# Rotary tables of units 2 to 7: by way of memory, two units at a time, or by spreading products on TensorE

## The chip, the cores and the metric

The kernel runs on one core of a Trainium2 chip. The core has five engines with instruction streams of their own: TensorE (PE; its weight loads are listed apart as PEld), VectorE (DVE), ScalarE (ACT), GpSimd (POOL) and SyncE (SP), which in this kernel issues every DMA. They share an on-chip memory of 128 partitions (SBUF) and a small accumulator memory for TensorE's results (PSUM, used here in banks of 512 numbers per partition). A DMA moves data between SBUF and the chip's memory, which the code calls DRAM; the core has 16 DMA engines. The metric is the device time of one execution in microseconds (us), the median of several runs; lower is better. All arithmetic is in 32-bit floats.

## The reference

The input x is 32 sequences of 64 tokens with 512 features. It passes two blocks. Block 0 is a rotary attention with 8 query heads of 64 features and one key and value head, followed by an MLP with a SiLU gate and 2048 inner features. Block 1 is a latent attention with 16 heads of 32 features. Both normalise their input and scale it by a product of the condition `cond_2048`. Cut to what matters for the change:

```python
def apply_rope(x, pos_ids):                       # block 0, HD = 64
    half = HD // 2
    inv_freq = 1.0 / ROPE_BASE ** (jnp.arange(0, HD, 2) / HD)      # 32 frequencies
    ang = pos_ids.astype(jnp.float32)[:, :, None] * inv_freq
    cos = jnp.concatenate([jnp.cos(ang), jnp.cos(ang)], axis=-1)[:, None]
    sin = jnp.concatenate([jnp.sin(ang), jnp.sin(ang)], axis=-1)[:, None]
    x1, x2 = (x[..., :half], x[..., half:])
    return x * cos + jnp.concatenate([-x2, x1], axis=-1) * sin

# block 0
h = ada_rms(x, time_emb, ln1_w, ln1_tw)
q, k = apply_rope(heads(h @ Wq.T), pos_ids), apply_rope(heads(h @ Wk.T), pos_ids)
x = x + softmax(q k^T / 8) v @ Wo.T
h = ada_rms(x, time_emb, ln2_w, ln2_tw)
x = x + (silu(h @ Wg.T) * (h @ Wu.T)) @ Wd.T
# block 1
x = x + latent_attention(layernorm(x) * (1 + scale) + shift) @ Wo.T
```

The positions are an input, so the cosines and sines have to be computed from them in the kernel: for each sequence, token and frequency one cosine and one sine.

## The kernel before, in words

**Units.** The 2048 tokens are worked on in 8 units of 256 tokens, four sequences each (`US` is 4, `S` is 64, `UT` is 256). A unit passes `attention0` (block 0's attention), `mlp` and `second`, which runs `attention1` (block 1). Features lie on the partitions and tokens along the free axis, so that a projection is a row of TensorE products with the weights as the stationary side.

**The MLP.** The inner features are worked on in 8 columns per unit, 64 columns q in all. For each there are three weight sets: m = 0 for the gate, m = 1 for up, m = 2 for down. Each product of a set is done by a scheme that needs seven block products in place of eight and some sums of blocks. `first_products` and `last_products` issue the products of gate and up (`product`, L937) and the sums of their results on DVE and ACT; `gated` makes the gated activations on DVE and POOL; `down` issues the products of the down set (L996). A set is a tile of [128, 7, 256] numbers in one of five buffers (`mw`). In unit 0 three of its seven blocks are loaded with one DMA (L251), one more with another (L254), the other four are summed from these on DVE and POOL (`combine`, L264 to L267) and written to memory (L272). From unit 1 on a set takes two loads, L251 (384 KB) and L256 (512 KB), which fetches those four blocks. The next set is asked for in `done_with`, when the last product of an older one has been issued, so its load waits on SP until that buffer is free.

**The rotary tables.** `angles(u0)` computes cosines and sines for two units at once from the positions: some two dozen DVE operations, two Sin activations on ACT and a last DVE product with a sign (L370). Its result, `angle` [128, 2, 512], stands by frequency and sequence: partition b·32 + f holds frequency f of sequence b of every unit, which leaves 64 tokens per unit along the free axis. The rotation needs something else: all 256 tokens of the unit along the free axis, and on every partition the frequency that belongs to its feature. `spread_out` makes this with four TensorE products with matrices of zeros and ones (L409), one for each sequence, which write a bank of PSUM. `tables(u, r)` calls it for units 2 to 7 and has DVE multiply the cosines (L418) and the sines with their sign (L419) with the normalisation `r` into a tile `cs`; these two operations read PSUM. Then `rotate` uses `cs` on the query and `attention0` on the keys. Units 0 and 1 have their own way (`first_angles`, `tables_by_quarters`), which stays as it is.

**When this happens.** The angles of units 2 and 3 are computed at the end of `attention0` of unit 1, those of 4 and 5 at the end of that of unit 3, those of 6 and 7 at the end of that of unit 5: they are passed as `late`, which `attention0` calls behind its last step. In the profiled execution the last operation of the angles ran at 85.4, 400.4 and 635.0 us, and the products of unit 2's tables began at 165.5 us, those of unit 7's at 771.8 us.

**The order.** Each job (the MLP of unit u, `attention0` of unit u + 1, the chain of `second`) is a generator that yields pairs of cost and latency. `Order.run` always takes the ready job that has done the smallest part of its total, so the costs in the yields decide how the steps of the jobs are interleaved. The order in which operations are issued is handed to the Tile framework, which orders each engine's stream by it and by its own priorities, and places tiles in SBUF, where tiles of different names can share memory at different times. An engine runs its stream in order. All DMAs stand in SP's one stream: weight sets, x, the sums of unit 0's sets, positions and results. A transfer that has to wait holds up those behind it.

Of the kernel before, what the change touches and what calls it, by code (L numbers as in the profile page):

```python
# [10 lines left out]
F32 = mybir.dt.float32  # L11
I32 = mybir.dt.int32
AF = mybir.ActivationFunctionType
ALU = mybir.AluOpType
# [3 lines left out]
P = 128  # L18
B, S, D = 32, 64, 512
# [3 lines left out]
US = UT // S  # L23
# [4 lines left out]
HD0, HALF0 = 64, 32  # L28
HD1, HALF1 = 32, 16
# [82 lines left out]
def two_blocks(ctx: ExitStack, tc: tile.TileContext, a: dict, out: bass.AP):  # L112
    nc = tc.nc
# [3 lines left out]
    dram = ctx.enter_context(tc.tile_pool(name="dram", bufs=1, space=bass.MemoryType.DRAM))  # L117
# [4 lines left out]
    def bank(tag, name):  # L122
        return psum.tile([P, 512], F32, tag=tag, name=name, bufs=BANKS[tag])
# [4 lines left out]
    def abank(name):  # L128
        tags = homes["now"]
        homes["n"] += 1  # L130
        return bank(tags[homes["n"] % len(tags)], name)
# [4 lines left out]
    def fixed(shape):  # L136
        n, i = int(np.prod(shape[1:])), stays["at"]
        stays["at"] += n
        assert stays["at"] <= STAY
        t = stays["all"][:, i : i + n]  # L140
        if len(shape) == 2:
            return t
        names = "abc"[: len(shape) - 1]
        return t.rearrange(f"p ({' '.join(names)}) -> p {' '.join(names)}", **dict(zip(names, shape[1:])))

    def work(tag, shape, name, bufs=2):
        return wk.tile(shape, F32, tag=tag, name=name, bufs=bufs)
# [19 lines left out]
    for q in range(US):  # L167
        rows = slice(q * HALF0, (q + 1) * HALF0)
        for i in range(2):
            block = ident[rows, rows][:, i * HALF1 : (i + 1) * HALF1].unsqueeze(1).unsqueeze(1)  # L170
            to = spread[rows, q].rearrange("p (r a h f) -> p r a h f", r=2, a=2, h=2)[:, :, i]
# [10 lines left out]
    def load_positions(u0):  # L182
        t = work("pos", [P, 2 * S], f"pos_{u0}", 1).bitcast(I32)
        nc.sync.dma_start(t, a["pos"][:, u0 * S : (u0 + 2) * S])
        positions.append(t)
# [9 lines left out]
    sign_of = small[:, C_SIGN:C_ALL]  # L195
# [12 lines left out]
    angle = fixed([P, 2, NU * S])  # L208
# [120 lines left out]
    def angles(u0):  # L329

        cols = slice(u0 * S, (u0 + 2) * S)

        def some(tag, name, cols=512, bufs=2):
            return work(tag, [P, cols], f"{name}_{u0}", bufs)[:, : 2 * S]

        posi = positions.pop()
        posf, sign = some("u", "posf"), some("v", "sign")
        ang, lo, hi = (some(f"ang{i}", f"ang{i}", 2 * S, 1) for i in range(3))
        prod = some("r0", "prod", UT, 1)
        acc, rnd = angle[:, 0, cols], angle[:, 1, cols]  # L340
        nc.vector.tensor_copy(posf, posi)
        nc.vector.tensor_scalar(sign, posf, 0.0, None, ALU.is_ge)
        nc.vector.tensor_scalar(sign, sign, 2.0, -1.0, ALU.mult, ALU.add)
        nc.vector.tensor_tensor(posf, posf, sign, ALU.mult)
        nc.vector.tensor_scalar(ang, posf, freq, None, ALU.mult)
        nc.vector.scalar_tensor_tensor(lo, ang, 4097.0, ang, ALU.mult, ALU.subtract)
        nc.vector.scalar_tensor_tensor(hi, ang, 4097.0, lo, ALU.mult, ALU.subtract)
        nc.vector.tensor_tensor(lo, ang, hi, ALU.subtract)

        def fraction(dst, src):  # L350
            nc.vector.tensor_scalar(rnd, src, ROUND, ROUND, ALU.add, ALU.subtract)
            nc.vector.tensor_tensor(dst, src, rnd, ALU.subtract)

        first = True
        for piece, turn in ((hi, 0), (hi, 1), (lo, 0), (hi, 2), (lo, 1)):
            nc.vector.tensor_scalar(prod, piece, TURN[turn], None, ALU.mult)
            if first:
                fraction(acc, prod)
                first = False
            else:  # L360
                fraction(prod, prod)
                nc.vector.tensor_tensor(acc, acc, prod, ALU.add)
        nc.vector.scalar_tensor_tensor(acc, lo, TURN[2], acc, ALU.mult, ALU.add)
        nc.vector.scalar_tensor_tensor(acc, ang, TURN[3], acc, ALU.mult, ALU.add)
        fraction(prod, acc)
        nc.vector.tensor_scalar(lo, prod, 0.25, None, ALU.add)
        fraction(hi, lo)
        nc.scalar.activation(acc, hi, AF.Sin, scale=TWO_PI)
        nc.scalar.activation(rnd, prod, AF.Sin, scale=TWO_PI)
        nc.vector.tensor_tensor(rnd, rnd, sign, ALU.mult)  # L370
        if u0 + 2 < NU:
            load_positions(u0 + 2)

# [32 lines left out]
    def spread_out(ps, of):  # L406

        for b in range(US):
            nc.tensor.matmul(ps[..., b, :], spread[:, b], of, start=True, stop=True)  # L409

    def tables(u, r):

        ps = abank(f"tab_{u}").rearrange("p (i b s) -> p i b s", i=2, s=S)
        spread_out(ps, angle[:, :, u * S : (u + 1) * S])
        cs = work("cs", [P, 2, UT], f"cs_{u}", 1)
        cos, sin = cs[:, 0], cs[:, 1]
        ps = ps.rearrange("p i b s -> p i (b s)")
        nc.vector.tensor_tensor(cos, ps[:, 0], r, ALU.mult)  # L418
        nc.vector.scalar_tensor_tensor(sin, ps[:, 1], sign_of, r, ALU.mult, ALU.mult)  # L419
        return cos, sin  # L420

    def tables_by_quarters(u, few, room):

        r = few[:, 0]
        nc.vector.tensor_tensor(
            few[:, 1:3], angle[:, :, u * S : (u + 1) * S], r.unsqueeze(1).to_broadcast([P, 2, S]), ALU.mult
        )
        ps = abank(f"tab_{u}").rearrange("p (i b s) -> p i b s", i=2, s=S)
        spread_out(ps, few[:, 1:3])
        pr = abank(f"row_{u}")[:, :UT]  # L430
        spread_out(pr.rearrange("p (b s) -> p b s", s=S), r)
        cs = work("cs", [P, 2, UT], f"cs_{u}", 1)
        ps = ps.rearrange("p i b s -> p i (b s)")
        nc.scalar.copy(cs[:, 0], ps[:, 0])
        nc.scalar.mul(cs[:, 1], ps[:, 1], sign_of)
        row = space(room, "r", UT, f"r_a{u}")
        nc.scalar.copy(row[HD0:], pr[HD0:])
        return cs[:, 0], cs[:, 1], row
# [14 lines left out]
    def space(room, tag, columns, name):  # L453

        if tag in room:
            return room[tag].pop(0)[:, :columns]
        if tag == "few":
            return work({"0": "tot0", "1": "kr1"}[room["ring"]], [P, columns], name, 1)
        return work(tag + room["ring"], [P, columns], f"{name}", RING.get(tag, RING.get(tag + room["ring"], 1)))
# [45 lines left out]
    def rms(u, s, h, room, name):  # L505

        x = x_units[u]
        lean = "lean" in room
        sq = tile4(room, "h", f"sq_{name}") if lean else work("sq", [P, KC, UT], f"sq_{name}", 1)
        nc.scalar.activation(sq, x, AF.Square)  # L510
        if lean:
            parts = [sq[:, k] for k in range(KC)]
            c = KC // 2
            for e, part in ((nc.vector, slice(0, c)), (nc.gpsimd, slice(c, KC))):
                to = h[:, part].rearrange("p c (b s) -> p c b s", s=S)
                of = x[:, part].rearrange("p c (b s) -> p c b s", s=S)
                by = s[:, part, US * u : US * (u + 1)].unsqueeze(3).to_broadcast([P, c, US, S])
                e.tensor_tensor(to, of, by, ALU.mult)
            yield 0.0, 1.5
        else:  # L520
            parts = [total_of(room, sq, name)]
            nc.gpsimd.tensor_tensor(by_seq(h), by_seq(x), per_seq(s, u), ALU.mult)
            yield 0.0, 6.0
        if lean:
            return parts
        r = space(room, "r", UT, f"r_{name}")
        inverse_root(mean_of(parts, f"ms_{name}"), eps0, r)
        return r
# [67 lines left out]
    def attention0(u, room, early=None, late=None):  # L596
        kb, vb = kblk0[u % 2], vblk0[u % 2]
        lean = "lean" in room
# [24 lines left out]
        r = yield from norm  # L623
# [9 lines left out]
        if lean:  # L633
            cos, sin, r = tables_by_quarters(u, few, room)
        else:
            cos, sin = tables(u, r)
        yield 1.0, 0.0

        qT = tile4(room, "qT", f"qT0_{u}")
        turn = turn or query(0)  # L640
# [34 lines left out]
        if lean:  # L675
            ps = [space(room, "p", 512, f"p0_{u}_{t}") for t in range(2)]
        else:
            both = space(room, "p", 1024, f"p0_{u}")
            ps = [both[:, t * 512 : (t + 1) * 512] for t in range(2)]

        for ts in ((0,), (1,)) if lean else ((0, 1),):
            banks = [abank(f"sc0_{u}_{ts[0]}_{r}")[:, : 256 * len(ts)] for r in range(2)]
            for n in range(KC * len(ts)):
                t, c = ts[n // KC], n % KC
                for b in range(2):
                    cols = slice((2 * t + b) * S, (2 * t + b + 1) * S)
                    for r, sc in enumerate(banks):
                        of = slice(r * HD0, (r + 1) * HD0)
# [7 lines left out]
            p = ps[ts[0]] if lean else both  # L696
# [39 lines left out]
        r = yield from rms(u, s0b, h, room, f"b{u}")  # L736
        if lean:
# [3 lines left out]
            r = abank(f"row_b{u}")[:, :UT]  # L741
# [512 lines left out]
```

## Time and profile before

Three runs took 1048.55, 1048.79 and 1049.76 us; the median is 1048.79. The profiled execution took 1047.82 us; its span, from the first to the last instruction, is 1046.0 us, at a mean granted TensorE clock of 0.992.

| engine | busy us | share of the span | instructions |
|---|---|---|---|
| PE | 1007.5 | 96% | 8578 |
| PEld | 936.4 | 90% | 8578 |
| DVE | 548.7 | 52% | 1379 |
| ACT | 334.1 | 32% | 683 |
| POOL | 436.4 | 42% | 521 |

| DMA | KB each | count | median us from issue to landing |
|---|---|---|---|
| set from `in_wmlp` | 384 | 192 | 4.7 |
| set from `sums` | 512 | 168 | 5.7 |
| sums from set | 512 | 24 | 4.8 |
| a from `in_wmlp` | 128 | 24 | 3.1 |

The DMA queue of SP carried 197.17 MB in 68752 packets, 54.5% of the time of the 16 DMA engines. A row of the groups gives the source line, the engine, the operation, the tile written and the tiles read, the shapes and the count, then the busy time and the mean duration in ns, then the idle time of the engine just before and what ended it. A matmul of 32-bit floats shows as two records.

### The profile page before, as it was taken

Reading aid. Unit: us, or ns where it says so; the run is one execution under the profiler, and the core shown is the slowest. Engines: PE = TensorE matmul, PEld = TensorE weight load, DVE = VectorE, ACT = ScalarE, POOL = GpSimd, SP = SyncE. Lnnn points to the kernel's source line nnn. Section 1 sums busy time; section 2 is a strip of 40 time slices with the busy share of each in tenths; the row PEclk is TensorE's granted clock in tenths of the full one; section 3 lists DMA queues with packets and bytes.
Section 4 is the critical chain, followed back from the end, with each engine's and each line's share of the span. In section 5 each row is a group of like instructions: output and inputs, shape, how many; then the busy total and the mean of one; then the engine's idle time right before and its main releaser. Section 6 shows DMA issues by size and latency. Waiting matters only on the chain.

```text
span 1046.0 us, 21558 instructions
## 1 busy us (share of the span) xinstructions
PE 1007.5 (96%) x8578; PEld 936.4 (90%) x8578; DVE 548.7 (52%) x1379; ACT 334.1 (32%) x683; POOL 436.4 (42%) x521
## 2 busy tenths in 40 slices
PE   7899999999999998999999999999999999999987
PEld 6679989998999998999999989899999899999875
DVE  4966656454355376444664366652465425543372
ACT  5333112244123242143340342242323512333141
POOL 3424545544244532445342354324553334642351
PEclk8989999999999999999999999999999999999999
DMA  8816886553655563673646646446745547565201
GB/s 279 314 60 202 275 299 244 195 175 144 230 198 185 171 213 125 233 247 104 229 163 231 233 141 212 160 155 219 259 165 193 180 167 250 185 235 202 79 1 40
DMA packets 68850, 198.53 MB, mean 190 GB/s; under 512 B 7312, under 2 KB 16272, under 8 KB 68368
## 3 DMA queue, kind: packets, MB, share of 16 engines
q1 hardware_dynamic: 68752, 197.17, 54.5%
q8 instruction: 68, 1.11, 0.4%
q14 instruction: 30, 0.25, 0.1%
HBM read 180.37 MB, written 16.78 MB: 188 GB/s over the span
## 4 chain that ended last, share of the span: by engine, by line
PE 81%; DVE 8%; POOL 4%; DMA 4%; issue 2%; ACT 1%; SPq 0%; ACTq 0%; DVEq 0%; POOLq 0%
PE gu L937 33%; PE down L996 16%; PE q L535 10%; PE po L535 10%; DMA set<-in_wmlp 3%; PE sc L875 2%; PE pp L570 1%; PE cx L902 1%; PE lat L535 1%; PE sc L689 1%; PE kv L535 1%; PE cx L710 1%; DVE set L264 1%; DVE sm L563 1%; DMA x<-in_x 1%
## 5 line engine op out<-in xcount | busy, mean ns | idle before, releaser
L937 PE MATMUL gu<-h,set 128*128 128x128 f32 x2048 | 288.6, 277 | 6.8 <-DVE c L956 6.3
L937 PEld LDWEIGHTS gu<-h,set 128*128 128x128 f32 x2048 | 259.4, 193 | 16.2 <-issue 11.3
L937 PE MATMUL gu<-hc,set 128*128 128x128 f32 x1536 | 215.7, 276 | 0.0
L937 PEld LDWEIGHTS gu<-hc,set 128*128 128x128 f32 x1536 | 193.9, 193 | 1.0 <-issue 0.6
L975 POOL TENSOR_TENSOR act<-c,c 128x384 f32<-128x384 f32 x64 | 66.4, 1037 | 212.1 <-DVE c L963 138.2
L996 PE MATMUL down<-td,set 128*128 128x128 f32 x1024 | 137.7, 276 | 3.7 <-POOL td L978 2.5
L996 PEld LDWEIGHTS down<-td,set 128*128 128x128 f32 x1024 | 125.5, 192 | 5.7 <-POOL td L978 3.5
L949 ACT COPY e<-gu 128x128 f32<-128x128 f32 x128 | 33.7, 264 | 260.9 <-PE gu L937 244.9
L535 PE MATMUL po<-cT,stays 128*128 128x256 f32 x480 | 109.4, 382 | 3.4 <-DVE x L583 1.8
L535 PE MATMUL q<-h,stays 128*128 128x256 f32 x480 | 109.4, 381 | 0.0
L996 PE MATMUL down<-act,set 128*128 128x128 f32 x768 | 109.4, 278 | 0.0
L963 DVE TENSOR_TENSOR c<-gu,u 128x256 f32<-128x256 f32 x128 | 53.4, 419 | 106.5 <-PE gu L937 106.2
L951 DVE TENSOR_TENSOR u<-e,gu 128x128 f32<-128x128 f32 x128 | 36.1, 282 | 129.7 <-ACT e L949 129.1
L535 PEld LDWEIGHTS po<-cT,stays 128*128 128x128 f32 x480 | 89.7, 192 | 15.9 <-DVE x L583 2.6
L996 PEld LDWEIGHTS down<-act,set 128*128 128x128 f32 x768 | 97.7, 192 | 5.3 <-issue 3.2
L535 PEld LDWEIGHTS q<-h,stays 128*128 128x128 f32 x480 | 90.1, 191 | 12.3 <-issue 0.4
L565 POOL TENSOR_TENSOR p<-p,sm 128x512 f32<-128x512 f32 x40 | 41.6, 1058 | 121.5 <-DVE sm L564 115.6
L546 POOL TENSOR_TENSOR qT<-u_q,v_q 128x512 f32<-128x512 f32 x30 | 38.1, 1270 | 89.0 <-DVE v_q L545 88.9
L1032 ACT ACT_TABLE_LOAD x35 | 44.9, 1283 | 55.6 <-DVE c L963 55.1
L589 DVE TENSOR_TENSOR x<-x,po 128x512 f32<-128x512 f32 x28 | 19.2, 687 | 72.9 <-PE po L535 72.9
L977 POOL TENSOR_TENSOR td<-act 128x256 f32<-128x256 f32 x64 | 46.7, 730 | 5.6 <-DVE act L974 0.9
L1032 ACT ACTIVATE c<-gu 128x128 f32<-128x128 f32 x64 | 17.7, 277 | 85.6 <-DVE c L963 77.7
(264 smaller groups left out, 1336.6 us busy)
## 6 DMA issues: line engine op xcount, KB each, us to landing
set<-sums SPq DMA_DIRECT2D x168, 512.0 KB, 5.7
set<-in_wmlp SPq DMA_DIRECT2D x192, 384.0 KB, 4.7
sums<-set SPq DMA_DIRECT2D x24, 512.0 KB, 4.8
x<-in_x SPq DMA_DIRECT2D x8, 512.0 KB, 5.6
mod<-in_mod SPq DMA_DIRECT2D x7, 512.0 KB, 5.4
a<-in_wmlp SPq DMA_DIRECT2D x24, 128.0 KB, 3.1
out_x<-x SPq DMA_DIRECT2D x12, 256.0 KB, 2.6
stays<-in_wo SPq DMA_DIRECT2D x2, 1024.0 KB, 8.0
```

Of the source, the lines that this page charges most:

```text
L535: nc.tensor.matmul(ps, w[:, k, cols], h[:, k, :], start=(k == 0), stop=(k == KC - 1))
L546: nc.gpsimd.tensor_tensor(dst, u, v, ALU.add)
L565: nc.gpsimd.tensor_tensor(p8, p8, sm.unsqueeze(2).to_broadcast(wide), ALU.mult)
L875: nc.tensor.matmul(sc[b * S : (b + 1) * S, j * P : (j + 1) * P], qT[of, j, cols], kb[of, 2 * t + b].rearrange("p g k -> p (g k)"), start=True,
L937: nc.tensor.matmul(ps, w[:, slot, k * P : (k + 1) * P], b[of][:, k], start=start and k == 0, stop=k == 1, skip_group_check=True)
L949: nc.scalar.copy(e, ps[:, 0])
L951: nc.vector.tensor_tensor(u2, e, ps[:, 1], ALU.add)
L963: nc.vector.tensor_tensor(c.rearrange("p (a b) t -> p a b t", b=2)[:, :, 1], ps[:, 2:4], u2.unsqueeze(1).to_broadcast([P, 2, HT]), ALU.add,)
L975: nc.gpsimd.tensor_tensor(act[:, 1:4], gate[:, 1:4], c[:, 1:4], ALU.mult)
L977: nc.gpsimd.tensor_tensor(td[:, 0:2], act[:, 1:3], act[:, 0:2], ALU.subtract)
L996: nc.tensor.matmul(sums_of[u][p][:, c], w[:, slot, c * P : (c + 1) * P], b[of], start=q % NP == 0 and i % 2 == 0 and c == 0, stop=q % NP = ...
L1032: nc.scalar.activation(gate[2][:, 0], gate[0][:, 0], AF.Silu)
```

## The change

`angles(u0)` now ends with a call of a new function, `spread_table(u0)`. It makes a tile in DRAM, `rows` [32, 2, 4, 128], with the frequency in front, and fills it with four DMAs, one for each sequence b, from the partitions b·32 to b·32 + 31 of `angle` (32 KB each). Then it reads the tile back with four DMAs of 128 KB into a work tile `table` [128, 2, 4, 128] in SBUF. Each of them fills 32 partitions: it takes 16 frequencies, and a leading dimension of step 0 repeats them for two copies. The reads follow the writes in memory, so the first of them has to wait until all four writes have landed. The table holds two units, 128 tokens for each of the four sequences.

`tables(u, r)` takes its half of this tile in place of the PSUM bank and no longer calls `spread_out`; the two DVE operations read SBUF, and their operands are rearranged to [128, 4, 64]. The step of `attention0` that follows has the planner's cost 0.0 in place of 1.0, except in the units 0 and 1. All new DMAs are issued by SP: 8 for two units, 24 in all.

```diff
@@ angles(u0)
         nc.scalar.activation(rnd, prod, AF.Sin, scale=TWO_PI)
         nc.vector.tensor_tensor(rnd, rnd, sign, ALU.mult)
+        spread_table(u0)
         if u0 + 2 < NU:
             load_positions(u0 + 2)
@@
+    spread_tables = {}
+
+    def spread_table(u0):
+
+        rows = dram.tile([HALF0, 2, US, 2 * S], F32, tag=f"table{u0}", name=f"table{u0}")
+        for b in range(US):
+            nc.sync.dma_start(rows[:, :, b], angle[b * HALF0 : (b + 1) * HALF0, :, u0 * S : (u0 + 2) * S])
+        t = work("table", [P, 2, US, 2 * S], f"table_{u0}", 1)
+        for i in range(4):
+            of = rows[i % 2 * HALF1 : (i % 2 + 1) * HALF1].rearrange("f i b s -> f (i b s)")
+            to = t[i * HALF0 : (i + 1) * HALF0].rearrange("p i b s -> p (i b s)")
+            nc.sync.dma_start(to, of.unsqueeze(0).to_broadcast([2, HALF1, 8 * 2 * S]))
+        for u in range(2):
+            spread_tables[u0 + u] = t[..., u * S : (u + 1) * S]
+
     def tables(u, r):
 
-        ps = abank(f"tab_{u}").rearrange("p (i b s) -> p i b s", i=2, s=S)
-        spread_out(ps, angle[:, :, u * S : (u + 1) * S])
+        ps = spread_tables.pop(u)
         cs = work("cs", [P, 2, UT], f"cs_{u}", 1)
         cos, sin = cs[:, 0], cs[:, 1]
-        ps = ps.rearrange("p i b s -> p i (b s)")
-        nc.vector.tensor_tensor(cos, ps[:, 0], r, ALU.mult)
-        nc.vector.scalar_tensor_tensor(sin, ps[:, 1], sign_of, r, ALU.mult, ALU.mult)
+        r, to = r.rearrange("p (b s) -> p b s", s=S), cs.rearrange("p i (b s) -> p i b s", s=S)
+        nc.vector.tensor_tensor(to[:, 0], ps[:, 0], r, ALU.mult)
+        nc.vector.scalar_tensor_tensor(to[:, 1], ps[:, 1], sign_of, r, ALU.mult, ALU.mult)
         return cos, sin
@@ attention0
-        yield 1.0, 0.0
+        yield 1.0 if lean else 0.0, 0.0
```

## The prediction

> **What bounds the kernel now.** I read the chain of waits first, then the groups of instructions, then the table by stage, and last the single DMAs and instructions around the three places where the change puts transfers. The first answer is the page of the kernel before, its engine totals and its chain:
>
> ```profile
> PE 1007.5 (96%) x8578; PEld 936.4 (90%) x8578; DVE 548.7 (52%) x1379; ACT 334.1 (32%) x683; POOL 436.4 (42%) x521
> PE 81%; DVE 8%; POOL 4%; DMA 4%; issue 2%; ACT 1%; SPq 0%; ACTq 0%; DVEq 0%; POOLq 0%
> ```
>
> TensorE is busy for 96% of the span and carries 81% of the chain, so an instruction taken from it inside the steady part should come off the end. The groups, with shapes kept apart, price what is removed and what reads it (total us, mean ns, idle before it):
>
> ```profile
> L409 PE MATMUL tab<-stays 128*128 128x128 f32 x48 | 6.3, 273 | 0.0
> L418 DVE TENSOR_TENSOR cs<-tab,r_a 128x256 f32<-128x256 f32 x6 | 2.5, 417 | 0.2
> L265 DVE TENSOR_TENSOR set<-set 128x256 f32<-128x256 f32 x22 | 10.5, 476 | 0.0
> ```
>
> 48 records in six units are eight records per unit, back to back with no idle before them: 6.3 us of pure TensorE time, 1.05 us a unit. The table by stage (window, its length, busy us and count of PE, PEld, DVE, ACT, POOL, granted clock, DMA share, GB/s) shows where a late weight load can hurt:
>
> ```profile
> 50.00:100.00 50.00, 47.31 (x428) 42.06 (x431) 33.10 (x94) 17.35 (x35) 17.13 (x19) 0.90 0.37 127
> 100.00:165.00 65.00, 61.96 (x566) 60.69 (x567) 37.96 (x112) 9.71 (x30) 29.80 (x41) 1.00 0.87 294
> 530.00:660.00 130.00, 127.65 (x1035) 119.66 (x1034) 73.75 (x185) 40.59 (x80) 55.96 (x65) 1.00 0.57 193
> ```
>
> PE loses 3.0 us between 100 and 165, where the DMA engines are 87% busy; later they have room. From 165 to 980 us PE idles 9.3 us in all (815 less the busy times of the windows). SP, which issues every DMA in order, stands nearly always for a weight buffer, as its waits say (us in total, times, longest):
>
> ```profile
> SPq L251 <- PE gu L937: 518.7, 117, 30.4
> SPq L251 <- PE down L996: 100.6, 59, 11.3
> ```
>
> So each set is asked for when its buffer falls free. How late that is: the down set of gate column 39 is issued at 640.39 us, lands at 645.10 and is first used by PE at 646.45; the timeline shows the issue and the use:
>
> ```profile
> 640.39 0.33 SPq L251 DMA_DIRECT2D set<-in_wmlp  x1
> ```
>
> ```profile
> 646.45 0.61 PE L996 MATMUL down<-act,set 128*128 128x128 f32 x4
> ```
>
> Its slack is 1.35 us. I took the slack of the other sets in the same way: the down sets of unit 0 have 3.18 us (issued 91.82, landed 94.85, used 98.03), then 1.91, 1.0, 1.3, 0.33, 0.2 and 1.61; the one issued at 416.46 has 3.45; gate and up sets 5 to 19.
>
> **What the Trainium skill says.** "DMA: Bandwidth & Descriptors", section "Why a DMA increments its semaphore by 16 and not by 1": a DMA runs on k engines, the largest k up to 16 that divides the slowest dimension of both access patterns, and on the lowest-numbered ones. Its section "Rules for kernel authors" draws the case at hand: a leading zero-stride broadcast of c copies "confines the whole DMA to at most c engines". The new read has a source of [2 copies, 16 frequencies, 1024 values], so k would be 2. No run here shows it: every load of before has 128 partitions outermost. Section "Queues, rings and completion order": each engine takes descriptors in ring order, so what SP issues later queues behind on those two engines; the trace of before shows no such case either. Section "Anatomy of one DMA — SWDGE (gpsimd) path" puts most of about 2 us fixed time into the write's receipt; the nearest row agrees, 128 KB of the a tile land 3.1 us after issue at the median.
>
> **The change, part by part.** Removed: four spreading products per unit in units 2 to 7, 6.3 us of PE; nothing of the kind replaces them on PE. Where PE is not waiting this is all gain: −6.3.
>
> The two DVE products that make cos and sin stay, and read SBUF in place of PSUM: 417 ns to at most the 476 ns of the SBUF-only row, +0.06 us times 12. DVE is half idle: 0, and 0.7 us if that cover is gone.
>
> Added per pair of units: four writes of 32 KB and four reads of 128 KB, 24 DMAs in all, all on SP. An issue costs SP about 0.33 us (the timeline row above): 2.6 us a pair, beside waits of hundreds. The first read must wait until all four writes have landed, and holds up whatever SP has behind it. Size: 0.64 MB a pair, 1.9 MB beside 197 MB. Spread over 16 engines a read is 8 KB per engine; on two it is 64 KB each, sixteen packets of 4,096 bytes, which last 159 ns each in the trace at the median: 2.54 us a read, 10.2 us for four, on the same two engines, and every later set load ends behind them. I take two engines (chance 0.65), and keep sixteen as the other end.
>
> First pair (units 2 and 3, angles done at 85.7 us). In the compiled order the four writes stand among the combines of the first weight sets, then read 0, then the down set with 3.18 us of slack, two more loads, then read 1; reads 2 and 3 come at about 155 us, behind the load of the set with 1.61. Read 0 can go at about 92.1 us, so that set is issued 0.7 late and lands 2 to 3 us late, beyond its slack only just; read 1 adds 2.54 us for the set with 1.91. Together I take 1.5 us of PE stall, between 0.5 and 3. For reads 2 and 3, the next sets have 5.0 to 7.0 us: 0.3, between 0 and 1.
>
> Second pair (units 4 and 5, angles done at 400.7). The table's memory is shared with small MLP tiles, free at about 403.5; reads follow at about 404 and end, with about 2 us of receipt, near 416.2 on two engines. The cos product ran at 413.50, so DVE stands up to 2.8 us with products of the MLP queued behind it. PE reaches the data of that column only at about 420: 0.8 us, between 0 and 2.
>
> Third pair (units 6 and 7, angles done at 635.3). The writes land at about 639.3; three reads go then, ahead of the down set above. Two engines take 7.6 us for them, to about 647.5, then the set's own share (eight packets of 3,072 bytes at 121 ns and eight of 4,096, 2.2 us) and the receipt: it lands near 650 instead of 645.1. Less its slack of 1.35, PE stalls 3.5 us, between 1.5 and 5.5.
>
> The planner gets 0.0 in place of 1.0 as the cost of that step, so in units 1 to 6 attention pieces stand at other places between MLP products (the order of unit 0's products up to its last columns and of the tail is unchanged), and an added Sin table load of 1.28 us falls on ACT, which is 32% busy. Bound: reordering can recover at most the 9.3 us that PE idles there; a loss is of the size of the largest such wait, 6.3 us for DVE's c products in the whole run. I take 0, and 2.5 either way.
>
> Sum: −6.3 + 1.5 + 0.3 + 0.8 + 3.5 = −0.2. On the profiled execution of 1047.82 us (span 1046.0) that is 1047.6; the median of runs lies 0.97 above that execution, so 1048.6.
>
> **Rivals.** Hidden transfers: the reads run on all engines, or the two engines drain sooner. Then read and set share the bandwidth, only SP's later issue at the third pair stays (0.8 us against the slack of 1.35): −6.3 + 0.8 = −5.5, 1043.3. For it: DMA share 0.57 in the third place. Against: the divisor rule.
>
> Slower, by backlog in unit 0: between 92 and 165 us the two engines have 13% of 65 us, 8.5 us, to spare, and the next down sets have 0.2 to 1.9 us. If the 5.1 us of reads 0 and 1 are never drained before the tightest set, PE pays 4.9 instead of 1.5: +3.2, 1052.0. It decides once this stretch costs over 3.8 us (with the other 4.6 that is the gain plus 2.1). For it: share 0.87 and slack 0.2; against: half of the engines' time is free just before 100.
>
> That the products removed were not on the path, so that nothing is gained and little lost, is hardly possible with 0.0 idle before them; it would also end near 1048.
>
> **How the numbers follow.** A change under 0.2%, 2.1 us, can't be told from none here. Balanced: 0.42, of that faster 0.13, same 0.18, slower 0.11 (reordering of 2.5 and stall bounds). Hidden: 0.36, of that faster 0.32, same 0.04. Backlog: 0.20, all slower. Not on the path: 0.02, same. Faster 0.45, same 0.24, slower 0.31. The range takes in the hidden case with half a us below it and the backlog with 2 us above for the third pair's upper bound: 1042.5 to 1054; the balanced case alone is 1045 to 1051.5.
>
> **What would show it.** Right: the tab rows of units 2 to 7 gone and PE's busy total 6.3 lower; reads that land 5 to 12 us after issue while loads of 512 KB issued with them land 2 to 5 us later than before; a PE wait on a set near 98 and near 646. Wrong: reads landing in 3 us (hidden), PE idle between 92 and 165 up by over 3.8 us (backlog), or new PE waits far from the tables, on DVE's or ACT's products (reordering).

## The result

The change made the kernel slower: 1068.05 us at the median (1065.39 to 1068.76) against 1049.28 us (1048.55 to 1050.27) for the kernel before in the same session, a ratio of 1.0175 with a 95% interval of 1.0161 to 1.0190. That is 18.8 us more. 1048.6 us had been forecast, with a range from 1042.5 to 1054.0; the time lies 14 us above its upper end.

### The profile page after: what moved, and what is told of

It reads as the page before. It is cut to its first block, busy times and chain, and to the rows that moved or that the text cites. A ratio compares the mean times of both kernels' runs of the same rounds, so it can differ in the third digit from the quotient of the medians.

```text
span 1066.6 us, 21366 instructions
## 1 busy us (share of the span) xinstructions
PE 1011.1 (95%) x8530; PEld 937.8 (88%) x8530; DVE 551.1 (52%) x1379; ACT 335.2 (31%) x684; POOL 436.2 (41%) x521
## 4 chain that ended last, share of the span: by engine, by line
PE 75%; DVE 10%; DMA 5%; POOL 4%; ACT 3%; issue 2%; SPq 1%; ACTq 0%; POOLq 0%; DVEq 0%
PE gu L952 30%; PE down L1011 15%; PE po L550 10%; PE q L550 9%; DMA set<-in_wmlp 4%; PE sc L890 2%; PE pp L585 2%; PE cx L917 1%; PE lat L550 1%; PE kv L550 1%; PE sc L704 1%; DVE sm L578 1%; DVE mx L570 1%; PE cx L725 1%; DVE v_q L560 1%
## 5 line engine op out<-in xcount | busy, mean ns | idle before, releaser
L952 PE MATMUL gu<-h,set 128*128 128x128 f32 x2048 | 292.8, 279 | 7.4 <-DVE c L971 4.2
L952 PEld LDWEIGHTS gu<-h,set 128*128 128x128 f32 x2048 | 262.0, 194 | 18.8 <-issue 11.8
L1011 PE MATMUL down<-td,set 128*128 128x128 f32 x1024 | 140.9, 280 | 9.1 <-POOL td L993 7.4
L1011 PEld LDWEIGHTS down<-td,set 128*128 128x128 f32 x1024 | 127.9, 195 | 12.0 <-POOL td L993 8.4
L1011 PE MATMUL down<-act,set 128*128 128x128 f32 x768 | 109.5, 278 | 10.2 <-DMA set<-in_wmlp 10.2
L1011 PEld LDWEIGHTS down<-act,set 128*128 128x128 f32 x768 | 98.2, 193 | 14.2 <-issue 9.6
```

Of the source, the lines that this page charges most:

```text
L952: nc.tensor.matmul(ps, w[:, slot, k * P : (k + 1) * P], b[of][:, k], start=start and k == 0, stop=k == 1, skip_group_check=True)
L1011: nc.tensor.matmul(sums_of[u][p][:, c], w[:, slot, c * P : (c + 1) * P], b[of], start=q % NP == 0 and i % 2 == 0 and c == 0, stop=q % NP = ...
```

## The profile after

The profiled execution has a span of 1066.6 us, 20.6 more than before. The page of the changed kernel, its engine totals and its chain, as for the kernel before:

```profile
PE 1011.1 (95%) x8530; PEld 937.8 (88%) x8530; DVE 551.1 (52%) x1379; ACT 335.2 (31%) x684; POOL 436.2 (41%) x521
PE 75%; DVE 10%; DMA 5%; POOL 4%; ACT 3%; issue 2%; SPq 1%; ACTq 0%; POOLq 0%; DVEq 0%
```

The 48 records of the spreading products are gone (8578 less 8530), yet PE's busy time rose by 3.6 us, and its share of the chain fell from 81% to 75%. So PE does less, takes longer over it, and waits. PE's waits in the changed kernel (us in total, times, longest):

```profile
PE down L1011 <- DMA set<-in_wmlp: 10.2, 3, 6.9
PE down L1011 <- POOL td L993: 7.4, 4, 3.4
PE gu L952 <- DVE c L971: 4.2, 6, 1.2
```

Before, PE never waited for a set's load in this list, and 2.5 us in all for POOL's differences. Three single waits, near 101, 434 and 665 us, make up most of it. The first and the last are on a weight set; the timeline of PE shows them (in brackets, the idle time before and what ended it):

```profile
101.32 1.22 PE L1011 MATMUL down<-act,set 128*128 128x128 f32 x4 [2.80 <-DMA set<-in_wmlp]
```

```profile
664.75 1.19 PE L1011 MATMUL down<-act,set 128*128 128x128 f32 x4 [6.86 <-DMA set<-in_wmlp]
```

The set that PE waited for at 664.75 is the one that the forecast named, the down set of column 39. This is what SP issued around it:

```profile
649.66 1.95 SPq L423 DMA_DIRECT2D table<-table  x3
651.71 0.37 SPq L251 DMA_DIRECT2D set<-in_wmlp  x1
652.12 0.43 SPq L256 DMA_DIRECT2D set<-sums  x1
652.60 0.64 SPq L423 DMA_DIRECT2D table<-table  x1
```

Three table reads, then the set. It was complete at 665.89, 14.2 us after the issue of its first load; before, this took 4.7 us. PE's first product needs only the first of the two loads, so its wait ended a little earlier, at 664.75. How the DMA engines spent this time shows in the DMA view of the changed kernel from 655 to 675 us, in 40 slices of half a microsecond: the mean busy share of all 16 engines in tenths, and the bandwidth.

```profile
DMA  9998999999999999521111111111111111298999
GB/s 238 295 340 256 322 266 268 252 256 254 250 250 266 209 315 240 154 94 55 49 49 49 49 57 57 47 49 51 49 47 51 51 47 57 68 184 221 336 311 387
```

From about 664 to 672 us the share is one tenth at some 49 GB/s (0.13 over the whole stretch in the table below): an eighth of 16 engines is two. So two engines work off what is left, and the sets' parts on the other fourteen are done. That is the picture expected of a read confined to two engines.

The second wait stems from the late table of unit 4. On DVE the cosine product waited 2.95 us for the read, and 10 us later PE waited for differences that POOL makes from what DVE had made late. POOL had idled 7.6 us until the rotated query came and was then busy without a break, from 427.06 us until these differences were done:

```profile
424.11 0.43 DVE L433 TENSOR_TENSOR cs<-table,r_a 128x256 f32<-128x256 f32 x1 [2.95 <-DMA table<-table]
```

```profile
434.21 1.05 PE L1011 MATMUL down<-td,set 128*128 128x128 f32 x7 [3.37 <-POOL td L993]
```

Last, the clock. The table by stage, with short windows around the three waits and one inside the last of them (columns as before; the clock is the third from the right):

```profile
100.00:108.00 8.00, 6.53 (x55) 5.87 (x56) 4.96 (x15) 0.44 (x2) 2.57 (x3) 0.57 0.55 199
433.00:441.00 8.00, 6.79 (x30) 5.87 (x31) 1.68 (x6) 0.40 (x1) 1.53 (x3) 0.79 0.00 0
658.00:664.00 6.00, 0.00 (x0) 0.00 (x0) 0.86 (x3) 0.20 (x1) 0.00 (x0) 0.75 0.94 234
664.00:672.00 8.00, 7.17 (x35) 6.94 (x36) 1.93 (x5) 0.40 (x2) 1.41 (x2) 0.55 0.13 51
666.00:668.00 2.00, 1.98 (x9) 2.00 (x10) 0.30 (x1) 0.37 (x1) 0.00 (x0) 0.50 0.13 53
```

Each of the three waits is followed by a stretch at half clock (until 108.0, 439.1 and 671.2 us), in which PE counts as busy and does half the work. The kernel before had none between 74 us and its end. The stretches with PE at work last some 16.6 us; half of that, 8.3 us, is most of the 10.9 us by which PE is busy longer here than in the kernel with the saving alone, below.

## The experiments

The theory from these profiles: the reads run on two DMA engines because their leading dimension has size two; weight loads issued behind them land late; PE waits, and then runs at half clock for a while. The rivals: SP itself is held up (by the wait for the writes and by the number of issues), whatever engines the reads use; or the new order of the steps, which the planner's cost and the table's memory bring, costs the time.

### Reads on sixteen engines

Each read of two copies is made as two reads of 16 rows, 24 reads instead of 12:

```diff
-        for i in range(4):
-            of = rows[i % 2 * HALF1 : (i % 2 + 1) * HALF1].rearrange("f i b s -> f (i b s)")
-            to = t[i * HALF0 : (i + 1) * HALF0].rearrange("p i b s -> p (i b s)")
-            nc.sync.dma_start(to, of.unsqueeze(0).to_broadcast([2, HALF1, 8 * 2 * S]))
+        for i in range(8):
+            of = rows[i // 2 % 2 * HALF1 : (i // 2 % 2 + 1) * HALF1].rearrange("f i b s -> f (i b s)")
+            to = t[i * HALF1 : (i + 1) * HALF1].rearrange("p i b s -> p (i b s)")
+            nc.sync.dma_start(to, of)
```

> The same change, but each read of 128 KB with its repeated source is made as two reads of 64 KB, each from 16 rows to 16 partitions without the repeat (24 reads in all instead of 12). Theory (the leading dimension of two confines each read to two DMA engines, and the weight sets issued later queue behind it there): reads land within 5 us, the down set behind them in the third pair lands within 7 us of its issue instead of 14, no PE wait over 1.5 us at the three places, and the clock stays whole there: 1043 to 1049 us. Rival (SP is held up by the wait for the writes and by the number of issues, whatever engines the reads use): not better than the change, 1060 us or more. Rival (the new order of the steps costs the time): 1055 us or more.

Measured: 1046.25 us, 0.9979 of the kernel before (0.9971 to 0.9987), as the theory expected. The loss is gone and a small gain is left. The line of the reads gives the time from issue to landing (shortest, median, longest), and the table by stage the third place:

```profile
DMA to landing us min/median/max: 2.0/4.0/5.2
```

```profile
640.00:655.00 15.00, 15.00 (x124) 14.64 (x123) 7.67 (x18) 5.33 (x10) 5.46 (x7) 1.00 0.84 277
```

PE is busy throughout, at full clock. The down set of column 39 landed 5.6 us after its issue (642.05 to 647.66), with three reads (of half the size) ahead of it. SP's waits for the writes and twice as many reads are in this kernel too, so the rival of SP's hold-up is out as the main cause. What the run changed is the shape of the reads as a whole; whether the repeat, the size of the leading dimension or the smaller size of each read matters was not taken apart.

### Transfers without the saving, and the saving without transfers

```diff
 # the kernel before, with the new transfers; tables() still spreads on PE
         nc.vector.tensor_tensor(rnd, rnd, sign, ALU.mult)
+        spread_table(u0)
```

> The kernel before with the writes and the narrow reads of the change added, and the spreading products kept: the table in memory is made and read back but nothing uses it. Theory (the narrow reads delay the weight sets): PE waits near 98 us for about 3 us and near 660 us for about 7 us, each followed by half clock; the wait behind the late table near 424 us is gone, since nothing reads it: 1058 to 1066 us. Rival (the new order of the steps, or DVE's wait for the table): within 4 us of the kernel before, 1048 to 1053.

```diff
 # the changed kernel, without its transfers
-        rows = dram.tile([HALF0, 2, US, 2 * S], F32, tag=f"table{u0}", name=f"table{u0}")
...
+        t = wo0[:, :2].rearrange("p k (b s) -> p k b s", s=2 * S)
```

> The change without its transfers: the spreading products are gone, and the two DVE operations read their tables from a weight tile that has long been in SBUF (so the rotation is by numbers that are not cosines and sines). Theory (the order of the steps costs nothing and the removed products are worth their 6.3 us): 1041 to 1045 us. Rival (the new order costs part of the time): 1050 us or more. That the products were not on the path: 1047 to 1050.

Transfers alone: 1063.97 us, 1.0145 (1.0127 to 1.0164), as the theory expected. PE's waits for sets are there as in the changed kernel, and the wait of 3.37 us for POOL is not:

```profile
PE down L1012 <- DMA set<-in_wmlp: 10.2, 3, 7.6
```

The saving alone: 1043.52 us, 0.9949 (0.9934 to 0.9965). Its page:

```profile
PE 1000.2 (96%) x8530; PEld 930.1 (89%) x8530; DVE 552.4 (53%) x1379; ACT 335.6 (32%) x684; POOL 436.6 (42%) x521
```

PE is busy 7.3 us less than before, and the span is 5.9 us shorter. So the products were on the path and worth nearly what was forecast, and the order of the steps, which this kernel shares with the changed one up to what the transfers do to it, takes little of it. The rival of the order is out.

The saving alone is also the ruler for the changed kernel. The table compares the first product on the down set of a column, in the profiles:

| column | before, us | changed, later by | saving alone, later by | difference |
|---|---|---|---|---|
| 0 | 87.9 | 0.33 | −0.54 | 0.87 |
| 1 | 98.0 | 3.29 | −0.54 | 3.83 |
| 2 | 109.1 | 6.75 | −0.54 | 7.28 |
| 8 | 176.7 | 7.28 | −2.53 | 9.81 |
| 24 | 424.2 | 5.98 | −4.28 | 10.26 |
| 25 | 441.1 | 10.75 | −4.50 | 15.25 |
| 38 | 633.6 | 11.28 | −4.32 | 15.60 |
| 39 | 646.4 | 18.30 | −4.31 | 22.62 |
| 40 | 664.8 | 20.78 | −5.21 | 25.99 |
| 63 | 981.5 | 20.71 | −5.98 | 26.69 |

The transfers of the first pair cost 8.9 us (up to column 8), of the second 5.3 (column 24 to 38), of the third 10.4 (38 to 40). Little is lost in between or behind. The waits themselves stand between columns 0 and 1 (3.0), 24 and 25 (3.4 of 5.0) and 38 and 39 (7.0). Directly behind them, where the clock is half, another 3.5 (columns 1 to 2), 1.6 and 3.4 us (39 to 40) are lost, 8.5 in all. Each column is one execution, and that of the saving alone was the fastest of five; by the two ratios the difference is some 24 us and not 26.7.

### One pair at a time

```diff
     def spread_table(u0):
+        if u0 not in (6,):        # (2,) and (4,) in the two other kernels
+            return
 # tables() spreads on PE for all other units, at the planner's old cost
```

> The change for units 6 and 7 alone; units 2 to 5 keep the spreading products. Theory (one down set behind three narrow reads): one PE wait of 5 to 8 us near 650 us, then some 7 to 10 us at half clock, less 2.1 us for the products saved: 1055 to 1061 us. Rival (the delays of the three pairs build up, the third alone is small): under 1052 us.

> The change for units 2 and 3 alone; the others keep the spreading products. Theory (narrow reads ahead of unit 0's down sets, wait and half clock): a PE wait of 2 to 4 us near 100 us and half clock behind it, later delays where reads 2 and 3 come, less 2.1 us: 1053 to 1057 us. Rival (most of the loss is in the other pairs): under 1051 us.

> The change for units 4 and 5 alone. Theory (a late table: DVE waits in front of the cosine product, POOL's differences and PE's down products come late): a PE wait of 2 to 4 us on POOL near 430 us, half clock behind it, less 2.1 us: 1049 to 1053 us. Rival (DVE's wait is covered): 1045 to 1048 us.

Units 6 and 7 alone: 1057.33 us, 1.0070 (1.0045 to 1.0096), as the theory expected. One wait for a set stands in its list:

```profile
PE down L1021 <- DMA set<-in_wmlp: 7.4, 1, 7.4
```

Units 2 and 3 alone: 1051.89 us, 1.0042 (1.0022 to 1.0062), between the two expectations. Its profile is of the fastest of six executions, 2.0 us below the median. There the wait is shorter than the 2.80 us in the changed kernel, and no half clock follows:

```profile
99.47 0.71 PE L1021 MATMUL down<-act,set 128*128 128x128 f32 x4 [1.99 <-DMA set<-in_wmlp]
```

Units 4 and 5 alone: 1051.51 us, 1.0037 (1.0023 to 1.0050), within the theory's range. In its profile, again of the fastest of six executions, DVE waits longer for the table than in the changed kernel and PE shorter for what comes of it. The half clock that was expected behind this wait does not come:

```profile
419.41 0.43 DVE L437 TENSOR_TENSOR cs<-table,r_a 128x256 f32<-128x256 f32 x1 [6.82 <-DMA table<-table]
```

```profile
426.66 1.60 PE L1021 MATMUL down<-td,set 128*128 128x128 f32 x12 [1.90 <-POOL td L1003]
```

The three ratios add up to 1.49%, against 1.75% for the change. So the delays come in three separate places and nearly add; they don't build up from one to the next, which was the rival for the third pair.

### The same narrow reads, behind the set

Again units 6 and 7 alone, but all four reads are ordered behind both loads of the down set of column 39:

```diff
             sets[n] = t
+            if n >= place[2, 39] and later:
+                with ordered_behind(tc):      # SP's order: after its last instruction
+                    later.pop()()             # the four reads of spread_table(6)
```

> The change for units 6 and 7 alone, as before, with the same four narrow reads, but SP issues all four behind both loads of the down set of column 39 in place of three ahead of them. Theory (what is issued later queues behind the reads on two engines): that set lands within 6 us of its issue, PE waits less than 1 us for it, no half clock follows; the sets behind the reads have 10 us of slack: 1045 to 1049 us. Rival (the reads slow everything in flight, whatever the order): PE still waits over 4 us near 650 us, 1053 us or more.

Measured: 1052.29 us, 1.0040 (1.0026 to 1.0055), between the two expectations. The set itself is as expected: issued at 641.01, landed at 646.28, and PE does not wait for it. But the loads behind the reads, issued at 644.84 to 646.50, landed 16 to 18 us later, more than their slack of about 10 us, and PE waited at another set:

```profile
661.27 0.72 PE L982 MATMUL gu<-h,set 128*128 128x128 f32 x2 [3.13 <-DMA set<-in_wmlp]
```

So order decides which load is late, as the theory says. The ratio falls from 1.0070 to 1.0040, with intervals that just overlap. The part of the theory that failed is that a slack of 10 us would cover what stands behind.

### What the half clock costs

The kernel with the transfers alone, with products of ones put where PE would stand idle:

```diff
+    FILL = {1: 4, 39: 12}         # then {1: 9, 39: 30}
 ...
         w, b = sets[place[2, q]], acts[q]
+        if q in FILL:
+            idle(FILL[q])
```

> The kernel before with the writes and narrow reads added and the spreading products kept, and with products of ones on PE, 4 ahead of the down products of column 1 and 12 ahead of those of column 39 (about 2.2 and 6.6 us), where PE would stand idle for the set. They compute nothing that is used. Theory (a wait costs its length and then half clock): the sets land as late as without them, but the clock stays whole, so PE gets back what half clock cost, some 3.4 us at the first place and 2 at the second: 1057 to 1061 us, against 1064 without them. Rival (the half clock costs nothing of its own): 1063 us or more.

The first size was wrong. The timeline of PE shows the 12 products at the second place (24 records) and what was left of the wait:

```profile
650.61 2.84 PE L161 MATMUL idle<-stays 128*128 128x128 f32 x24
658.44 1.19 PE L1015 MATMUL down<-act,set 128*128 128x128 f32 x4 [4.98 <-DMA set<-in_wmlp]
```

24 records took 2.84 us, 0.12 each, though each lasts 275 ns: they overlap. The time was 1063.86 us, 1.0146 (1.0130 to 1.0162), no gain. With more of them:

> As the filled kernel above, but with 9 and 30 products of ones in place of 4 and 12, since the trace shows that they take 0.11 us a record and not 0.27: about 2.0 and 6.7 us of PE time, close to the whole waits of 2.5 and 7.8. Theory: no half clock at either place, the second included (half clock from 657 to 664 us is gone), 1057 to 1061 us against 1064. Rival (the half clock has nothing to do with the waits, or costs nothing): 1063 us or more.

Now the waits are filled, and the clock stays whole, as the windows around the second place show, first with the transfers alone and then filled:

```profile
659.00:667.00 8.00, 4.98 (x31) 5.01 (x32) 0.88 (x3) 0.37 (x1) 0.00 (x0) 0.61 0.33 102
```

```profile
656.00:660.00 4.00, 3.18 (x29) 2.99 (x27) 0.00 (x0) 0.00 (x0) 0.00 (x0) 1.00 0.74 194
660.00:668.00 8.00, 7.35 (x61) 7.17 (x62) 2.71 (x8) 3.52 (x6) 3.13 (x4) 1.00 0.45 126
```

That the half clock at these places follows from the wait is shown: with the loads as late as before and PE kept at work, it does not come. But the time was 1063.24 us, 1.0154 (1.0139 to 1.0169), not distinguishable from the 1.0145 without filling. The expected 1057 to 1061 did not come.

The profiles show more. Without filling, columns 1 to 2 and 39 to 40 took 3.9 and 1.6 us longer than in the kernel before, 5.5 in all. Filling brought 2.8 us of that back (14.90 against 12.81 us from the first product on the down set of column 1 to that of column 2, 19.93 against 19.22 for 39 to 40). At full clock PE came upon the next late load, the second one of the set of column 39:

```profile
660.06 0.68 PE L1015 MATMUL down<-act,set 128*128 128x128 f32 x4 [0.88 <-DMA set<-in_wmlp]
661.33 0.91 PE L1015 MATMUL down<-td,set 128*128 128x128 f32 x6 [0.59 <-DMA set<-sums]
```

And the filled kernel has a stretch at half clock elsewhere, from 401.0 to 404.4 us behind a wait of 1.74 us, which the unfilled one with the same wait has not; its lead fell there from 3.1 to 1.9 us (columns 22 to 23). The end moved from 1063.6 to 1060.9 us, and single executions differ by as much. So the half clock's own cost in this kernel is some 3 us of 17 by the profiles, and not shown by the times of the runs.

### Versions that keep the change

```diff
 # wide46: the wide reads for units 4 to 7; units 2 and 3 spread on PE
+        if u0 not in (4, 6):
+            return
 # wide_cost1: the wide reads for all three pairs, the planner's cost as before
-        yield 1.0 if lean else 0.0, 0.0
+        yield 1.0, 0.0
```

> The wide reads for units 4 to 7; units 2 and 3 keep the spreading products, so that unit 0, where the DMA engines are fullest, has no new transfers. Theory (of the wide version's gain some 2 to 3 us were lost to waits in unit 0 and at its end): 4.2 us of products saved, little given back: 1043 to 1046.5 us. Rival (the other pairs gave it back): 1046.5 to 1049.

> The wide reads for all three pairs, with the planner's cost of the step left at 1.0 as in the kernel before. Theory (the order of steps moves single waits of 1 to 3 us about and no more): within 3 us of the wide version's 1046, 1043 to 1049. Rival (the changed cost is what costs the wide version its last microseconds): 1044 us or less.

The first: 1046.30 us, 0.9988 (0.9978 to 0.9998). Leaving the first pair on PE brings nothing over the wide reads everywhere. The second: 1043.99 us, 0.9968 (0.9956 to 0.9980), 3.4 us faster than the kernel before and faster than the changed kernel by some 22 by the two ratios. By the ratios it is 1.2 us faster than the wide version with the changed cost, and the intervals overlap. Its profile has one stretch at half clock between 75 us and its end, where that of the version with the changed cost has two (behind waits of 2.91 us at 172.9 and 1.93 us at 254.2). Its time fits the theory and, at 1044 us or less, the rival as well; whether the old cost is the better choice here the runs do not settle.

## Why the prediction was wrong

**The saving** of 6.3 us was right: 5.3 us in the runs of the saving alone (3.7 to 6.9), 5.9 in its profile.

**Two engines** was right as the likelier end. The rule in the Trainium skill, "DMA: Bandwidth & Descriptors", section "Rules for kernel authors" (a leading repeat of c copies keeps a DMA on at most c engines), holds here: the share of one tenth in the view of the DMA engines, 49 GB/s, and the wide reads agree with it. The forecast's source for the receipt is a section on transfers that GpSimd issues; here SP issues them, and the writes of 32 KB landed 1.9 to 2.5 us after issue. All three places were named, two with the right wait and the right set. The sum failed in its sizes: 1.5 + 0.3 for the first pair, 0.8 for the second, 3.5 for the third, 6.1 in all, where the difference to the saving alone shows 8.9, 5.3 and 10.4. Two terms failed: the waits, which were priced too short, and the half clock behind them, which was put at nothing.

**Third pair.** "Two engines take 7.6 us for them" was priced by packets of 4,096 bytes at 159 ns. In the changed kernel such packets lasted 254 ns at the median between 654 and 664 us, and those of 3,072 bytes 180 instead of 121. With 254 ns throughout, an estimate, three reads are 12.2 us instead of 7.6, and the set's share 3.5 instead of 2.2: 5.9 us more. From 664 to 672 us, when two engines worked alone, the packets took 162 and 125 ns. So the price failed while reads and set loads kept all 16 engines busy together, and held for the two engines by themselves. In the other direction, the slack of 1.35 us was counted to the landing of the set's second load. The first, for which PE waits, landed in the kernel before at 643.84 and left 2.6 us. The wait was 6.86 us, the forecast 3.5 with 5.5 as its upper end.

**First pair.** "That set is issued 0.7 late" was too little. An issue of a write took 0.57 to 0.67 us and of a read 0.59 to 0.71, not 0.33, and the read waited for the writes until 93.69 us instead of 92.1. The set was issued at 94.47, 2.7 us later than before, of which PE's own delay is 0.3; and it landed 6.8 us after issue instead of 3.0. The issues, before and after:

```profile
91.82 3.15 SPq L251 DMA_DIRECT2D set<-in_wmlp  x3
```

```profile
93.69 0.71 SPq L423 DMA_DIRECT2D table<-table  x1
94.47 1.30 SPq L251 DMA_DIRECT2D set<-in_wmlp  x3
```

That took all of the slack of 3.18 us and a wait of 2.80. The half clock behind it took 3.5 us. About 2.5 us more were lost up to column 8, in smaller waits, the longest 1.14 us for DVE at 168.90.

**Second pair.** DVE's wait came as forecast, 2.95 us for 2.8. The step that failed is "PE reaches the data of that column only at about 420": it asked when PE gets to this column, and not what stands behind the waiting product on DVE. The sums of the current MLP column and the keys were queued there, POOL was late and fully busy in turn, and PE's wait was 3.37 us instead of 0.8.

**The clock** was left out of the sum, though stalls of up to 5.5 us were forecast. In the profile of the changed kernel the time lost at half clock directly behind the three waits is 8.5 of the 20.6 us by which 26.7 exceeds 6.1. How much of it PE would have lost at full clock, in waits for the next late loads, stays open: filling gave back 2.8 of 5.5 us in the profiles and nothing that the times of the runs show.

**The rivals.** The one that ended slower had the first pair's backlog as its place, 4.9 us; the third pair was larger. It had the right sign and a sixth of the size. The 8.5 us that it gave the two engines to spare are 13% of the 65 us from 100 to 165 us, not of the 73 us from 92. The hidden case did not come in this kernel; with the 16-row reads, whose loads were not held up, the time of 1046.25 us lies 3 us above the 1043.3 forecast for it. The upper end of the range added only the third pair's upper bound to the backlog, and the loss at each of the three places then came out beyond its upper end (3 and 1, 2, and 5.5).

## What to carry to other kernels

Look at the leading dimension of a DMA first: here reads with a repeat of two in front kept 128 KB on two of the 16 engines, and the set loads issued later waited for those two. When such a transfer is priced, price what stands behind it on the same queue against its slack, with the packet times seen while both are in flight, add the clock behind each wait, and ask of each waiting instruction what is queued behind it on its engine. A saving on the bounding engine is worth its busy time only if the work that replaces it stays out of the way of that engine's loads; here the same change with 16-row reads kept a third to two thirds of it.

## What was not expected of the hardware

- While narrow reads and set loads were in flight together, from 654 to 664 us, the packets were slower (254 and 180 ns at the median against 159 and 121), and the sixteen engines showed as busy at some 250 GB/s, where the kernel before, in slices as full, often moved 350 to 430. Once two engines were left, they took 162 and 125 ns, though by the order of issue one narrow read was still among their work. With 16-row reads, from 640 to 650 us, they took 162 and 125 ns as well. Why, the runs do not say.
- Behind 75 us, half clock came with each of the nine single waits of PE from 2.31 to 7.62 us in the profiles of all these kernels, and not with one of 2.22 us and one of 1.99 us. Shorter ones went either way. With a wait of 1.93 us near 255 us it came in the two wide versions for all pairs and in the first filled kernel, and not in the kernel before or with the saving alone. With one of 1.74 us between 394 and 404 us it came in four kernels, and not with the transfers alone. The stretches lasted 3.4, 6.8 or 10.2 us.
- Matmul records of 275 ns follow each other every 0.11 to 0.12 us (60 in 6.86 us), so the mean duration of a row is no price for a number of them; the row's busy time is.
